# An offset of its own in the schedule's keys for each of a group's 16 steps

## Chip, cores and metric

The kernel runs on one core of a Trainium2 chip. The metric is the time of one execution on the device in microseconds (us). Of the kernel before there are three runs: 2164.63, 2165.2 and 2167.5 us; the median is 2165.2.

## What is computed

The input is a batch of 128 graphs of 64 nodes with 512 features each, and a weighted adjacency matrix of 64x64 for each graph. Four layers follow one another, each of the form x = layernorm(x + layer(x, adj)):

```python
# layer 0: A = exp(leaky(8 tanh((s_i + s_j) / 8))) * adj, rows normalized; A @ x @ w
# layer 1: softmax-like attention over the graph: adj * exp(q k^T), rows normalized, times v
# layer 2: w_i = q_i . (adj @ k)_i / sqrt(512); softmax over the graph; times v
# layer 3: hypergraph convolution 512 -> 1024, relu, layernorm, hypergraph convolution 1024 -> 512
x = _layernorm(x + _L0_gnn_ref(x, adj, L0_gnn_w, L0_gnn_a), axis=-1)
x = _layernorm(x + _L1_gnn_ref(x, adj, ...), axis=-1)
x = _layernorm(x + _L2_gnn_ref(x, adj, nodemask, L2_gnn_Wqk, L2_gnn_Wv), axis=-1)
x = _layernorm(x + _L3_gnn_ref(x, adj, ...), axis=-1)
```

All of it is in fp32.

## The kernel before

Two graphs make a tile of 128 rows, two tiles a group; there are 32 groups, and two groups share a chunk of adjacency data. A group goes through all four layers without leaving the chip: only x comes in and the result goes out. The products with the weights are made by Strassen's scheme (seven half-size products, `seven_products`, with the sums of the left side made by DVE in `side_sums`); the weight pieces are prepared once, stored in DRAM, and streamed back for every group into a ring of eight buffers of 512 KB.

The kernel does not write instructions in the order of its code. `run(g)` (line 1004) only records operations with `order.add` (line 76): the engine, an estimated cost, what is read and written, and a key. `step(k)` (line 1006) sets the key for the operations of the 16 steps of a group, numbered 0 to 15: layer 0 is steps 0 to 2 (scores and their exponentials, the gather over the graph, the products), layer 1 is 3 to 6, layer 2 is 7 to 11, layer 3 is 12 to 15. `BASE[g]` sets the groups apart by 4 key units, so that the 16 units of one group overlap those of the next three.

`keys_by_what_follows` (line 105) then replaces the step by a finer one: an operation's place is computed from the longest chain of work that follows it in its group, on a scale of 16 units. What the operation had been given ahead of its step is kept: `urgent` (100 for `NOW`, the operations that empty a PSUM bank, 1.5 for the weight streams) and `early`:

```python
        o.engine, o.cost, o.emit, o.key, o.step = engine, cost, emit, self.key - urgent - self.early, self.key
                urgent = o.step - o.key
                o.key = o.step - urgent
```

`Order.run` (line 140) is a list scheduler. It keeps, for each engine, a heap of the operations whose inputs are ready by its own estimate, and takes the one with the lowest key for which buffers are free: 14 of the kind k4 (activations), 8 of the ring, 8 PSUM banks, 7 of e and so on, each a stack of free numbers. It allows eight DMAs under way (`UNDERWAY`), and a group's loads no further than `AHEAD` in front of the work. For TensorE `choose` (line 122) also looks at the tiling mode: some matmuls use the whole array, others four quarters of 64x64 (`mode="quarters"`: the gathers over a graph) or two columns (`mode="columns"`: the scores); it stays in a mode while the keys are not too far apart. The sum over a graph (`over_graph`, line 968) may be written whole or in halves, as the mode just then is.

The order in which operations are taken is then the order in which they are emitted, and it is fixed for every engine by dependencies between neighbours (`pinned`, line 1172). Each engine works through its own queue strictly in that order, and SyncE, which issues every DMA, too. So the keys decide, before anything runs, in what order each of the five queues stands, and which buffer number each operation uses. All instructions carry the line of this helper, 1178, in the profile; they are told apart by the names of their buffers.

Before the change, only the operations of step 0 have an offset: `EARLY = 1.0`, set in `run` around step 0 and taken back ahead of step 1.

The first group also prepares the weights: `prepare_first` makes the pieces of w0 and of layer 1's v in the ring buffers, uses them in place for group 0, and stores them to DRAM; from group 1 on `streamed` loads them from there.

Of the kernel before, what the change touches and what calls it, by code (L numbers as in the profile page):

```python
# [28 lines left out]
BASE = [APART * g - 2 * min(g, 4) - 2 * max(g - NG + 3, 0) for g in range(NG)]  # L29
# [29 lines left out]
class Order:  # L59
# [4 lines left out]

    NEAR, FAR = 0.5, 4.0
    ENOUGH = 48
    EARLY = 1.0

    BLOCK, REST = 64, 3500
    AHEAD = 3.5  # L70
# [189 lines left out]
def kernel(  # L260
# [51 lines left out]
    order = Order({k: len(v) for k, v in kinds.items()})  # L312
# [10 lines left out]
    def dve(n, reads, writes, emit, urgent=0.0, port=None):  # L323

        if port is None:
            port = all((b[0] if isinstance(b, tuple) else b).kind != "bank" for b in reads)
        order.add("DVE", w_dve(n), reads, writes, emit, urgent, port=port)
# [55 lines left out]
    def load_x(g):  # L383
        order.key = (-11.0, -10.3)[g] if g < 2 else BASE[g] - 6.0
        xs[g] = Buf("x", 4)
        load(xs[g], x_g[g], P * GT * D * 4)

    def load_adj(c):
        order.key = BASE[GC * c] - 7.0 if c else -10.5
        adjs[c] = Buf("adj")  # L390
        load(adjs[c], adjT[:, ts(c, CT * N)], P * CT * N * 4, lambda t_: t_.rearrange("p t i -> p (t i)"))

        turned = turned_adjs[c] = Buf("adj", 2 * GT)
        order.key += 0.0 if c else 0.6
        for t in range(GT):
            for h in range(2):
                dma(P * 256, [], [turned[2 * t + h]],
                    lambda t=t, h=h: turned.t[ts(t, N)].rearrange("p (g h) i -> p g h i", h=2)[:, :, h],
                    lambda t=t, h=h: adjT_c[c, t][:, :, h])
# [604 lines left out]
    def run(g):  # L1004

        def step(k):
            order.key, order.group = BASE[g] + float(k), g

        step(0)
        xt = xs.pop(g)  # L1010
        adj, turned, gm, am, sums, g1, dc, dh = prepared[g // GC]
# [2 lines left out]
        of_x = lambda t: xt[[2 * t, 2 * t + 1]], lambda t: xt.t[:, t, :]  # L1014


        order.early = order.EARLY
        s = Buf("col", GT)
        diag, e, ps_s = Buf("e", GT), Buf("e", GT), Buf("bank")
        for t in range(GT):  # L1020
# [4 lines left out]
        for t in range(GT):  # L1025
# [8 lines left out]
        rs = Buf("e")  # L1034
        dve(7 * GT * N, [ps_e], [rs], lambda: nc.vector.reciprocal(flat(rs.t), ps_e.t[:, : GT * N]), NOW)
        dve(GT * N, [e, rs], [e], lambda: nc.vector.tensor_mul(e.t, e.t, rs.t))
        order.early = 0.0
        step(1)
        left = left_side(gathered(*of_x, lambda h, t: e.t[halves[h][0], t, :], [e]))
        step(2)  # L1040
        seven_products(*left, first_use["w0"] if g == 0 else streamed("w0"), *scaled_into(
            at_x, sums, slice(2 * CT + own.start, 2 * CT + own.stop), D // 2))
# [116 lines left out]
    for g in range(NG):  # L1159
        if g:  # L1160
            load_x(g)
        if g % GC == 0:
            if g:
                load_adj(g // GC)
            prepare_chunk(g // GC)
        run(g)
        order.group = None


    last, names, behind = {}, {}, []  # L1170
# [78 lines left out]
```

## Time and profile before

| what | value |
|---|---|
| median of three runs | 2165.2 us (2164.63 to 2167.5) |
| the profiled execution's own time | 2166.22 us |
| its span, first to last instruction | 2164.4 us |
| TensorE, mean granted clock | 0.998 |
| instructions | 51412 |
| DMA traffic | 476.34 MB, mean 220 GB/s |

The profile is of one execution. "PE" is TensorE's matmuls, "PEld" its weight loads, which lie beside the matmuls; "SPq" is SyncE's queue, which issues the DMAs. An fp32 matmul stands as two records, so a product of 256 columns over two blocks of 128 rows is four records of 128x256. Buffer names tell what an operation is for:

| out<-in | what it is |
|---|---|
| bank<-ring,k and bank<-ring,h | products with a streamed weight piece |
| bank<-k,m | products with the two Gram matrices m1 and m2 that stay on chip |
| bank<-ident,x | transposes |
| bank<-e,x, bank<-kept,x, bank<-kept,h | gathers over a graph, in quarters |
| bank<-k,k 128*64 | scores, in columns |
| bank<-k,k 128*128 | making of the Gram matrices, at the start only |
| bank<-e,same | sums over a graph |

The costliest groups of TensorE, with their number, busy time and mean duration of one:

| group | number | busy us | mean ns |
|---|---|---|---|
| bank<-ring,k 128x256 | 3456 | 801.3 | 382 |
| bank<-k,m 128x128 | 3584 | 437.0 | 276 |
| bank<-ring,k 128x512 | 512 | 237.6 | 598 |
| bank<-ring,h 128x256 | 1024 | 235.2 | 380 |
| bank<-ring,h 128x512 | 384 | 176.8 | 594 |
| bank<-kept,h 64x64 | 4096 | 74.1 | 221 |
| bank<-k,k 128x64 | 2048 | 74.2 | 225 |

Matmuls overlap in the records, since each is drawn from its start to its modelled end; so the mean durations are longer than the distance from one start to the next.

### The profile page before, as it was taken

Reading aid. Unit: us, or ns where it says so; the run is one execution under the profiler, and the core shown is the slowest. Engines: PE = TensorE matmul, PEld = TensorE weight load, DVE = VectorE, ACT = ScalarE, POOL = GpSimd, SP = SyncE. Lnnn points to the kernel's source line nnn. Section 1 sums busy time; section 2 is a strip of 40 time slices with the busy share of each in tenths; the row PEclk is TensorE's granted clock in tenths of the full one; section 3 lists DMA queues with packets and bytes.
Section 4 is the critical chain, followed back from the end, with each engine's and each line's share of the span. In section 5 each row is a group of like instructions: output and inputs, shape, how many; then the busy total and the mean of one; then the engine's idle time right before and its main releaser. Section 6 shows DMA issues by size and latency. Waiting matters only on the chain.

```text
span 2164.4 us, 51412 instructions
## 1 busy us (share of the span) xinstructions
PE 2142.8 (99%) x20831; PEld 1717.2 (79%) x20831; DVE 1541.9 (71%) x3967; ACT 856.9 (40%) x1812; POOL 386.1 (18%) x399
## 2 busy tenths in 40 slices
PE   7999999999999999999999999999999999999998
PEld 4887777887888787887878887878877888878866
DVE  6777767677776776776777776777766777766675
ACT  2444343343433433443433434434334333343433
POOL 1113121021201212101222111212012211012120
PEclk9999999999999999999999999999999999999999
DMA  8866668666666667665666665666666666655475
GB/s 276 309 217 224 210 203 282 224 218 235 223 210 205 207 218 240 212 218 198 204 234 220 226 200 207 212 235 224 212 203 210 221 232 213 212 189 207 160 256 198
DMA packets 174364, 476.34 MB, mean 220 GB/s; under 512 B 35824, under 2 KB 45360, under 8 KB 174128
## 3 DMA queue, kind: packets, MB, share of 16 engines
q1 hardware_dynamic: 174128, 473.05, 64.4%
q8 instruction: 165, 2.70, 0.5%
q14 instruction: 71, 0.58, 0.1%
HBM read 443.33 MB, written 29.66 MB: 219 GB/s over the span
## 4 chain that ended last, share of the span: by engine, by line
PE 97%; DMA 2%; DVE 0%; ACT 0%; SPq 0%; issue 0%; POOL 0%; POOLq 0%; DVEq 0%; ACTq 0%
PE bank L1178 97%; DMA x<-in_x_dram 0%; DMA k<-in_wk_dram 0%; DMA ring<-in_wv_dram 0%; DMA k<-in_wqk_dram 0%; DMA v<-ring 0%; DMA ring<-w 0%; SPq L1178 0%; ACT k L1178 0%; DVE k L1178 0%; ACT x L1178 0%; DVE x L1178 0%; DVE col L1178 0%; POOL ring L1178 0%; POOLq L1178 0%
## 5 line engine op out<-in xcount | busy, mean ns | idle before, releaser
L1178 PE MATMUL bank<-ring,k 128*128 128x256 f32 (+1 forms) x3968 | 1035.4, 410 | 7.0 <-DMA ring<-w 4.9
L1178 PEld LDWEIGHTS bank<-ring,k 128*128 128x128 f32 x3968 | 730.3, 190 | 211.3 <-issue 111.2
L1178 ACT COPY k<-bank 128x512 f32<-128x512 f32 (+1 forms) x640 | 304.6, 501 | 603.3 <-PE bank L1178 405.7
L1178 DVE SCALAR_TENSOR_TENSOR x<-bank,col,x 128x256 f32<-128x256 f32 (+1 forms) x832 | 400.7, 500 | 198.8 <-PE bank L1178 187.4
L1178 PEld LDWEIGHTS bank<-k,m 128*128 128x128 f32 x3584 | 427.2, 192 | 22.2 <-issue 13.5
L1178 PE MATMUL bank<-k,m 128*128 128x128 f32 x3584 | 437.0, 276 | 0.0
L1178 PE MATMUL bank<-ring,h 128*128 128x256 f32 (+1 forms) x1408 | 412.0, 439 | 0.0
L1178 POOL TENSOR_TENSOR col<-col,mhalf 128x2 f32<-128x2 f32 (+1 forms) x161 | 111.4, 692 | 1476.8 <-DVE col L1178 634.0
L1178 PEld LDWEIGHTS bank<-ring,h 128*128 128x128 f32 x1408 | 260.1, 190 | 90.0 <-issue 64.3
L1178 ACT ACTIVATE x<-x,col,col 128x512 f32<-128x512 f32 x256 | 197.3, 809 | 168.7 <-DVE col L1178 168.5
L1178 DVE TENSOR_TENSOR k<-bank,k 128x256 f32<-128x256 f32 x384 | 154.0, 421 | 129.1 <-PE bank L1178 123.2
L1178 DVE BATCH_NORM_STATS2 col<-x 128x6 f32<-128x512 f32 x256 | 175.3, 688 | 4.5
L1178 DVE SCALAR_TENSOR_TENSOR h<-bank,col,b3a_b 128x512 f32<-128x512 f32 x128 | 95.9, 750 | 70.5 <-PE bank L1178 69.9
L1178 ACT ACTIVATE k<-bank,u_c 128x128 f32<-128x128 f32 x256 | 80.0, 364 | 133.2 <-PE bank L1178 131.7
L1178 ACT ACTIVATE h<-h 128x512 f32<-128x512 f32 x128 | 80.6, 631 | 127.5 <-DVE h L1178 127.4
L1178 ACT ACTIVATE h<-h,col,col 128x512 f32<-128x512 f32 x128 | 96.8, 807 | 73.6 <-DVE col L1178 73.6
L1178 DVE TENSOR_TENSOR k<-k 128x256 f32<-128x256 f32 x226 | 95.8, 425 | 41.0 <-ACT k L1178 40.6
L1178 PEld LDWEIGHTS bank<-k,k 128*64 128x64 f32 (+1 forms) x2112 | 77.3, 140 | 51.4 <-DVE k L1178 24.2
L1178 PE MATMUL bank<-k,k 128*64 128x64 f32 (+1 forms) x2112 | 105.7, 237 | 6.7 <-DMA k<-in_wk_dram 4.8
L1178 DVE SCALAR_TENSOR_TENSOR h<-bank,col,h 128x512 f32<-128x512 f32 x128 | 93.3, 748 | 22.7 <-PE bank L1178 20.6
L1178 POOL TENSOR_TENSOR x<-x,bv_b 128x512 f32<-128x512 f32 x64 | 81.1, 1271 | 92.0 <-PE bank L1178 68.4
L1178 POOL TENSOR_TENSOR k<-k,b3b_b 128x512 f32<-128x512 f32 x64 | 81.3, 1270 | 79.1 <-DVE k L1178 31.4
(96 smaller groups left out, 1494.4 us busy)
## 6 DMA issues: line engine op xcount, KB each, us to landing
ring<-3a SPq DMA_DIRECT2D x224, 512.0 KB, 4.6
ring<-3b SPq DMA_DIRECT2D x224, 512.0 KB, 4.4
ring<-v SPq DMA_DIRECT2D x189, 512.0 KB, 3.8
ring<-w SPq DMA_DIRECT2D x93, 512.0 KB, 3.3
x<-in_x_dram SPq DMA_DIRECT2D x32, 512.0 KB, 4.6
ring<-v SPq DMA_DIRECT2D x63, 256.0 KB, 4.0
out_dram<-x SPq DMA_DIRECT2D x31, 512.0 KB, 3.0
ring<-w SPq DMA_DIRECT2D x31, 256.0 KB, 4.1
```

The lines of the kernel that those rows point to most:

```text
L1178: made = f(*args, **kwargs)
```

## The change

The single offset becomes a list of 16, one for each step. `step(k)` sets it together with the key; the two lines that set and cleared it around step 0 go, and it is set to 0 after each group, so that the loads and the preparation of chunks, which are recorded between the groups, have none, as before. A positive offset lowers the keys of a step's operations, so that they are taken earlier among those ready; a negative one raises them.

```diff
-    EARLY = 1.0
+
+    EARLY = [2.22, 0.44, 0.0, 0.0, 0.0, 0.0, 0.0, 0.17, 0.0, 0.57, -0.17, -0.03, -1.1, -0.36, 0.0, -0.35]
...
         def step(k):
-            order.key, order.group = BASE[g] + float(k), g
+            order.key, order.early, order.group = BASE[g] + float(k), order.EARLY[k], g
...
-        order.early = order.EARLY
         s = Buf("col", GT)
...
         dve(GT * N, [e, rs], [e], lambda: nc.vector.tensor_mul(e.t, e.t, rs.t))
-        order.early = 0.0
         step(1)
...
         run(g)
-        order.group = None
+        order.early, order.group = 0.0, None
```

Nothing else differs: the operations, their costs in the scheduler, the buffers and their numbers are the same.

## The prediction

> **What bounds the kernel now.** I read the page's busy line and its chain first, then the idle time of TensorE by what ended it, then one table of six stretches, then the timeline at the start and the end.
>
> ```profile
> PE 2142.8 (99%) x20831; PEld 1717.2 (79%) x20831; DVE 1541.9 (71%) x3967; ACT 856.9 (40%) x1812; POOL 386.1 (18%) x399
> PE 97%; DMA 2%; DVE 0%; ACT 0%; SPq 0%; issue 0%; POOL 0%; POOLq 0%; DVEq 0%; ACTq 0%
> ```
>
> TensorE is busy 2142.8 of 2164.4 us and the chain is TensorE's own for 97%. The next engine, DVE, is at 71%.
>
> ```profile
> PE bank L1178 <- DMA ring<-w: 4.9, 1, 4.9
> PE bank L1178 <- DMA k<-in_wk_dram: 4.8, 2, 4.1
> PE bank L1178 <- DMA k<-in_wqk_dram: 1.8, 1, 1.8
> PE bank L1178 <- ACT k L1178: 1.7, 3, 1.2
> ```
>
> The six stretches (us, then busy time and instructions of PE, PEld, DVE, ACT, POOL, then clock, DMA share, GB/s):
>
> ```profile
> 0.00:62.00 62.00, 49.45 (x334) 28.86 (x335) 36.81 (x104) 16.77 (x49) 11.09 (x17) 0.94 0.87 286
> ...
> 400.00:1000.00 600.00, 600.00 (x5903) 484.38 (x5902) 430.80 (x1114) 237.20 (x498) 106.13 (x110) 1.00 0.65 218
> ...
> 2100.00:2165.00 65.00, 55.66 (x550) 42.22 (x548) 39.69 (x84) 22.54 (x36) 8.93 (x10) 0.98 0.58 197
> ```
>
> The first block holds TensorE's waits of over 1 us in total. In the stretches the second number after the colon is TensorE's busy time: 600.00 of 600.00 us in the steady part, 12.5 us short in the first 62, 9.3 short in the last 65, of which 7.7 lie after the last matmul's end at 2157.3 (0.6 of it beyond the span). A new order of the same work can therefore gain only at the two ends, and on whatever the steady 2000 us contain besides matmuls: changes of tiling mode.
>
> The timeline of TensorE at the start (start us, us, what, idle before it):
>
> ```profile
> 49.02 1.13 PE L1178 MATMUL bank<-ring,k 128*128 128x256 f32 x4
> 55.02 2.04 PE L1178 MATMUL bank<-ring,k 128*128 128x256 f32 x4 [4.86 <-DMA ring<-w]
> 56.85 0.63 PE L1178 MATMUL bank<-e,same 128*128 128x128 f32 x2
> 57.97 2.71 PE L1178 MATMUL bank<-ring,k 128*128 128x256 f32 x8 [0.48 <-DVE k L1178]
> 60.52 1.04 PE L1178 MATMUL bank<-ident,x 128*128 128x128 f32 x8
> ```
>
> The chain at the same place (start us, us, what), and the last matmuls of the timeline:
>
> ```profile
> 35.28 6.92 DMA ring<-in_wv_dram
> ...
> 42.45 1.70 POOL ring L1178
> ...
> 44.16 5.33 DMA v<-ring
> ...
> 49.51 0.59 SPq L1178
> ...
> 50.21 4.67 DMA ring<-w
> ```
>
> ```profile
> 2130.05 0.69 PE L1178 MATMUL bank<-kept,h 64*64 64x64 f32 x32
> 2131.96 1.99 PE L1178 MATMUL bank<-ring,k 128*128 128x256 f32 x8 [1.22 <-ACT k L1178]
> ```
>
> In the timeline TensorE stands 4.9 us before group 1's first product, until the weight piece w0 is back from DRAM at 54.88. The chain tells why that load is so late: the DMA queue on SyncE goes on only at 49.51, when the store of the v pieces has landed. In the last two lines a gathered block goes straight into a product, which waits for ACT's copy of it.
>
> **What the Trainium skill says.** "TensorEngine Tiling (Array Packing)", Key Properties: a change of tiling mode drains TensorE. The trace agrees, in start-to-start intervals: a 128x256 matmul takes 216 ns before another of its kind and 309 before one on divided tiles (+93); the last 64x64 one takes 148 ns before an undivided one, 38 before another divided shape (+110); columns to quarters is 152 against 38 (+114). "Perfetto Trace Analysis", Identifying the Most-Contended Engine: matmul busy share does not tell the distance to the roofline. It holds here too: a matmul of 382 ns mean starts every 216, so I count intervals, not busy time. "DMA: Bandwidth & Descriptors", Anatomy of one DMA: DMA engines don't wait on semaphores, the issuing sequencer does; the waiting SyncE queue at 44.16 to 49.51 is such a case.
>
> **The change, part by part.** No work is added or removed. By instruction count ACT (1814), DVE (3901), POOL (404) and SyncE (1073) hold the same number in both programs, TensorE one fewer: one over-graph sum more is written whole instead of as two halves. What moves is the order on all five queues, everywhere: step 0 of a group is keyed 2.22 early (1.0 before), step 1 0.44 and step 9 0.57 early, step 12 1.1 late, 13 and 15 some 0.35 late. A key's unit is a quarter of a group, about 17 us of TensorE (2120 us by 32 groups by 4). I price it where TensorE's time can change.
>
> 1. Mode changes. Counted in the two orders: before, 132 entries into divided tiles, 132 exits, 68 changes between columns and quarters; after, 131, 131 and 63. That is 93 + 110 + 5 x 114 = 773 ns. Gain 0.8 us.
>
> 2. The start. SyncE's first 36 issues are the same, and the 18 between there and the first reload of w0 are the same transfers in another order, behind the same v store (which needs POOL's 1.70 us at 42.45). One difference: the fourth x load now stands behind that store instead of ahead of it, and the reload eight transfers behind the x load, where the trace of before shows the queue standing for a transfer of about that distance. I put the landing 0.6 us later, at 55.5 (bounds: 0 and 1.2). What TensorE does ahead of it grows by four transposes (8 records x 112 ns = 0.9 us) and some small sums, together 1.0 us. Is that work ready? The w0 product that stood at 49.02 moves ahead of the last Gram matrix, to about 45; from its end, two DVE evictions (0.88), statistics (0.69 + 0.18 + 0.17), POOL's power (0.72), DVE's product and ACT's normalization (0.8 for a tile), with the DVE work queued between, end near 52.6; transposing ends before 54. Yes. After the landing, before loses 0.34 at 55.57, 0.79 at 57.97 and 0.37 at 58.56 because operands of group 1 come from DVE late; in the new order the transposes and a gather stand there and DVE's side sums are several instructions earlier. I take all of these 1.5 us as gone (bounds 0.5 and 1.5). Gain 1.0 + 1.5 - 0.6 = 1.9 us. The earlier offset also frees the adjacency buffer for chunk 1's load, which before used a fresh one: its last reader, DVE's product for group 1, now comes near 30 us, the load at 36, so SyncE doesn't wait.
>
> 3. The steady part. Before has no wait there, so nothing can go; new ones can come. The ring of eight weight buffers has one tight place in the new order: near 327 and 333 us the same ring buffer is reloaded with 4.7 and 4.3 us of matmuls between its last use and its next. A load costs a wait of 0.1 to 0.3, an issue, and a median of 3.3 to 4.6 us to landing from the page's issue table: 4.9 taken. Loss 0.2 + 0.6 = 0.8 us (bounds 0 and 2). Beyond it TensorE's operands have as much matmul work between maker and user as before, mostly more. DVE at 71% and POOL at 18% are reordered beneath that cover; if the cover failed, each late operand would cost about the 0.4 to 1.2 us that such waits cost at the ends.
>
> 4. The end. In the new order five products (1.7 us each) stand between the gather of group 62 and the product that reads it: the 1.28 us at 2131.96 go. What is late next: group 63's last gather now follows its last 3a product after six products, 10.4 us, where before it had 12.4. The chain in between (two evictions to +1.8, relu to +2.9, statistics waiting behind residual adds to +7.1, POOL to +8.05, ACT's four pieces from +8.35, 0.73 each) has its first piece at +9.2 and the last at +11.3; the gather reads them at 10.4 to 12.0. It holds, by some 0.3 us for the second piece. The 7.1 us after the last matmul have the same instructions. Gain 1.3 us (bounds 0.6 and 1.7).
>
> Sum: -0.8 - 1.9 + 0.8 - 1.3 = -3.2 us. The profiled execution took 2166.22 (span 2164.4), 1.0 over the median of 2165.2; against the median 2165.2 - 3.2 = **2162.0**, 0.15% less. A measurement of this kernel can tell about 0.2% (4.3 us) from no change.
>
> **Rivals.**
> A, the forecast, 2162.0, chance 0.57, own range 2160.5 to 2164.
> B, the reload of w0 is earlier: if it need not wait for the x load or the store, SyncE could issue it when it reached it, near 47.9 instead of 50.2. Then 2.3 + 0.6 more are gained: 2162.0 - 2.9 = 2159.1. For: its own data were stored long before. Against: the chain shows the queue standing, and the transfers ahead are the same. Chance 0.22.
> C, the start gives nothing: the landing slips 1.2 us and new short operand waits follow it. 2162.0 + 1.9 + 0.6 = 2164.5. For: DVE is full there (36.8 of 62 us), and one of its v subtractions now stands ahead of three evictions and waits for a load. Chance 0.14.
> D, slower: the ring loads fall behind in every group, not in one place. Steps 13 and 15 start their streams with 0.35 less lead; if one load a group is late by the 0.3 us that separate a 4.6 us landing from the tight gap, 28 steady groups lose 8.4: 2162.0 + 8.4 = 2170.4. It decides from 7.5 us in sum, or 0.27 a group. Against: loads and their users are shifted by the same offset, steady DMA share is 0.65, and before has not one ring wait after 55 us. Chance 0.07.
> That the change does nothing is excluded: the planner recomputes each key from what follows but keeps the offset, and the orders differ from the first matmuls of group 1 on.
>
> **How the numbers follow.** Faster: B and the lower edge of A, 0.22 + 0.04 = 0.26. Slower: D, 0.07. Same: 0.67. The range runs from below B, 2158.5, to 2166: C and A's bad bounds (2162.0 + 1.2 + 1.0 + 0.7 + 0.6 = 2165.5) are in it, D is out.
>
> **What would show it.** Mode changes: 325 in the trace. Start: the wait for the w piece is still the longest of TensorE, between 54.5 and 56, with transposes ahead of it, and nothing over 0.4 us behind it. Steady: short waits on the ring near 330 us and nowhere regularly. End: no wait of over 0.5 us after 2100. A regular wait in the steady part, or a w piece that lands before 53, would make the forecast wrong.

## The result, and the profile after

| | before | after |
|---|---|---|
| median | 2165.15 us (10 runs, 2164.63 to 2167.5) | 2159.56 us (10 runs, 2157.94 to 2163.08) |
| ratio to before, 95% interval | | 0.9973 (0.9965 to 0.9982) |
| profiled execution, span | 2166.22, 2164.4 us | 2158.29, 2156.5 us |
| changes of tiling mode in the trace | 332 | 325 |

The kernel is 5.6 us faster, 0.26%, and the interval of the ratio does not reach 1. The two profiled executions differ by 7.9 us: before's lies 1.0 over its median and after's 1.3 under its own. So some 2 us of what follows belong to the two executions and not to the change.

Busy line and chain of the kernel after:

```profile
PE 2139.4 (99%) x20829; PEld 1721.0 (80%) x20829; DVE 1529.5 (71%) x3967; ACT 861.1 (40%) x1812; POOL 385.7 (18%) x399
PE 97%; DMA 2%; DVE 0%; SPq 0%; ACT 0%; issue 0%; DVEq 0%; ACTq 0%
```

TensorE is still the bound, and its busy time fell by 3.4 us for the same matmuls. That is the first oddity: another order can take waits away, but why should the matmuls themselves get shorter? TensorE's waits of the kernel after (us in total, times, longest):

```profile
PE bank L1177 <- DVE e L1177: 1.7, 1, 1.7
PE bank L1177 <- DMA ring<-w: 1.5, 1, 1.5
PE bank L1177 <- DMA k<-in_wqk_dram: 1.3, 1, 1.3
PE bank L1177 <- DVE k L1177: 0.6, 1, 0.6
```

The wait for group 1's piece of w0 went from 4.9 us to 1.5, a wait of 1.7 us for DVE is new, and the last wait of over 1 us for ACT's copy is gone. The first and the last stretch (us, busy time and instructions of PE, PEld, DVE, ACT, POOL, then clock, DMA share, GB/s):

```profile
0.00:62.00 62.00, 52.35 (x428) 32.01 (x429) 39.17 (x113) 19.52 (x56) 11.98 (x18) 1.00 0.90 295
...
2100.00:2157.00 57.00, 49.40 (x435) 37.45 (x433) 33.59 (x76) 17.67 (x27) 7.70 (x9) 0.98 0.62 209
```

The number to look at is the clock: 1.00 in the first 62 us, where the same stretch of before had 0.94. That digit stood in the prediction's own fence and was not read. The timeline of TensorE at the start (start us, us, what, idle before it):

```profile
47.94 1.11 PE L1177 MATMUL bank<-e,x 64*64 64x64 f32 x60
50.75 0.44 PE L1177 MATMUL bank<-e,same 64*64 64x128 f32 x4 [1.70 <-DVE e L1177]
51.12 0.66 PE L1177 MATMUL bank<-ident,x 128*128 128x128 f32 x4
53.23 1.13 PE L1177 MATMUL bank<-ring,k 128*128 128x256 f32 x4 [1.45 <-DMA ring<-w]
54.20 0.60 PE L1177 MATMUL bank<-ident,x 128*128 128x128 f32 x4
```

One standstill of 4.9 us has become two of 1.7 and 1.5, with a sum over a graph and four transposes between them. The four matmuls with w0 take 1.13 us; in the kernel before the same four took 2.04. The end of the timeline:

```profile
2134.95 2.10 PE L1177 MATMUL bank<-kept,h 64*64 64x64 f32 x128
2137.27 3.72 PE L1177 MATMUL bank<-ring,k 128*128 128x256 f32 x16 [0.23 <-ACT k L1177]
```

The wait of 1.28 us behind a gather is gone, and the last gather costs 0.23, as it did before.

To see why matmuls got shorter, the clock has to be read in finer stretches. Before, from 52 to 60 us:

```profile
52.00:56.00 4.00, 0.98 (x2) 0.83 (x3) 2.25 (x7) 0.55 (x2) 0.72 (x1) 0.58 0.88 286
56.00:60.00 4.00, 3.52 (x11) 2.72 (x10) 2.08 (x7) 2.21 (x5) 0.00 (x0) 0.57 0.95 358
```

After, the same stretches:

```profile
52.00:56.00 4.00, 2.77 (x73) 2.39 (x74) 2.39 (x6) 1.06 (x3) 1.97 (x2) 1.00 1.03 370
56.00:60.00 4.00, 4.00 (x23) 3.65 (x23) 2.52 (x7) 2.24 (x6) 1.27 (x1) 1.00 0.98 357
```

In the kernel before, TensorE was granted half its clock from 52.63 to 59.46 us: from inside the long wait to 4.4 us behind it. A 128x256 matmul there starts 427 ns after the one before it, where the usual distance is 216 ns. Added up over the matmuls of that piece this is 1.9 us, besides 0.8 us of a wait for DVE among them. The profile of after has no such piece until its matmuls have ended. Another 0.6 us of the 3.4 is the half clock with which every execution begins: it lasted to 8.26 us before and to 7.24 after, while TensorE's first 49 matmuls stand in the same order in both kernels, so this part is no gain of the change.

The Trainium skill describes this under "TensorE: Matmul & The Clock Gate", What's actually happening: the clock is set half or full by how busy the array was in a free-running window of 3413 ns. The traces agree on the window: in this case's runs half-speed pieces between the start and the end last 3.41, 6.83 or 10.24 us, one to three windows. They differ on what sets it off. The page says an idle window; here windows in which TensorE was busy for up to 46% of the time (counted from its records) were followed by half speed, another of 46% and all above it were not, and a half-speed window had to be busy for somewhere between 81% and 86% for full speed to come back.

### The profile page after: what moved, and what is told of

Its sections match the earlier page's. It is cut to its first block, busy times and chain, and to the rows that moved or that the text cites. A ratio compares the mean times of both kernels' runs of the same rounds, so it can differ in the third digit from the quotient of the medians.

```text
span 2156.5 us, 51432 instructions
## 1 busy us (share of the span) xinstructions
PE 2139.4 (99%) x20829; PEld 1721.0 (80%) x20829; DVE 1529.5 (71%) x3967; ACT 861.1 (40%) x1812; POOL 385.7 (18%) x399
## 4 chain that ended last, share of the span: by engine, by line
PE 97%; DMA 2%; DVE 0%; SPq 0%; ACT 0%; issue 0%; DVEq 0%; ACTq 0%
PE bank L1177 97%; DMA x<-in_x_dram 0%; DMA k<-in_wk_dram 0%; DMA mask_rows<-e 0%; DMA k<-in_wqk_dram 0%; DMA ring<-in_wv_dram 0%; DMA ring<-w 0%; SPq L1177 0%; DVE x L1177 0%; DVE col L1177 0%; DVE ring L1177 0%; ACT x L1177 0%; DVE e L1177 0%; ACT k L1177 0%; DVE k L1177 0%
## 5 line engine op out<-in xcount | busy, mean ns | idle before, releaser
L1177 PEld LDWEIGHTS bank<-k,m 128*128 128x128 f32 x3584 | 432.8, 192 | 30.5 <-issue 19.9
L1177 PE MATMUL bank<-k,m 128*128 128x128 f32 x3584 | 445.9, 276 | 0.0
L1177 PE MATMUL bank<-ring,h 128*128 128x256 f32 (+1 forms) x1408 | 421.8, 440 | 0.0
L1177 DVE BATCH_NORM_STATS2 col<-h 128x6 f32<-128x512 f32 x128 | 87.3, 686 | 20.2 <-ACT h L1177 20.0
```

The source lines that it names most:

```text
L1177: made = f(*args, **kwargs)
```

## The experiments

Before and the variants were timed on the same chip in each of three sessions; before's medians there were 2165.54, 2165.09 and 2165.20 us. Each ratio is to before beside it. "Waits" below is the sum of all delays of over 60 ns in TensorE's starts, against the usual distance for that pair of matmuls, in one profile; matmuls at half clock count in it.

### Where the gain lies: the start, the middle and the end alone

Three kernels use the new list for some groups, and before's offset for the others:

```diff
-            order.key, order.early, order.group = BASE[g] + float(k), order.EARLY[k], g
+            order.key, order.group = BASE[g] + float(k), g
+            order.early = order.EARLY[k] if g <= 3 else float(k == 0)
```

In the second the condition is `g >= 28`, in the third `4 <= g <= 27`.

> The new offsets in groups 0 to 3 only, the single offset of 1.0 in the rest. Theory (the gain is mostly the start: less waiting of TensorE up to 62 us): 330 mode changes (0.2 us less than before), the start as in the changed kernel (3 to 4 us less), the end as before with its wait of 1.2 us: 2161.5 us. Rival (the gain is in the steady part, or in the mode changes alone): nothing to speak of is gained in four groups, 2164.9 us.

> The new offsets in groups 28 to 31 only. Theory: the start as before, 334 mode changes (0.2 us more), the wait of 1.2 us near the end gone because five products stand between the gather and its reader: 2164.0 us. Rival (the end is worth more than its one wait): 2162 us or less. Rival (the steady part): 2165.2 us.

> The new offsets in groups 4 to 27 only; the first 163 rows of TensorE's order are those of before, and the end again has the gather read at once. Theory: 329 mode changes, 0.3 us less, and nothing else: 2164.8 us. Rival (the steady part holds the gain): 2160 us. A new late ring load in the steady part would show as over 2165.5 us.

| new list for | median us | ratio (95%) | waits, first 60 us | waits, 2100 to 2150 us |
|---|---|---|---|---|
| groups 0 to 3 | 2165.65 | 1.0004 (0.9996 to 1.0012) | 11.4 | 2.5 |
| groups 28 to 31 | 2163.02 | 0.9990 (0.9983 to 0.9997) | 10.8 | 0.6 |
| groups 4 to 27 | 2165.47 | 0.9996 (0.9988 to 1.0005) | 12.4 | 2.3 |
| all (after) | 2159.56 | 0.9973 (0.9965 to 0.9982) | 8.4 | 0.6 |
| none (before) | | | 13.8 | 2.4 |

The two columns of waits are of one execution each: that for groups 0 to 3 took 3.6 us more than its kernel's median, the next two took 1.5 and 1.4 less than theirs. And 3.5 to 5.1 us of the waits of the first 60 us (5.1 before, 3.5 after) lie ahead of TensorE's 50th matmul, near 25 us, up to which its order is the same in all five. At both ends the groups also stand closer than was described: `BASE` sets the first five, and the last three, 2 units apart and not 4, so an offset is a larger share of their distance there.

The end is as predicted in kind: the 1.28 us go with the last four groups alone. The middle does nothing that can be measured. The start alone missed its theory by 4 us and met the rival, but not for the rival's reason: its trace shows a loss elsewhere. Timeline of TensorE in that kernel:

```profile
169.87 1.12 PE L1178 MATMUL bank<-k,ones 128*128 128x512 f32 x2 [1.12 <-DVE k L1178]
172.36 1.68 PE L1178 MATMUL bank<-k,m 128*128 128x128 f32 x8 [1.37 <-DVE k L1178]
```

and the stretch behind it, with the clock as third number from the end:

```profile
173.00:176.00 3.00, 3.00 (x16) 3.00 (x16) 1.59 (x6) 1.12 (x2) 0.00 (x0) 0.50 0.84 343
```

At 170 us DVE still prepares layer 3's weights, once. TensorE's order leaves that of the kernel after at 89 us, ahead of this preparation, DVE's operands came late twice, and the half clock followed: 5.7 us of waits between 160 and 300 us, where before has 1.3. So the experiment had made a loss of its own, though this execution, 3.6 us over the median, shows more of it than most.

### The start alone, with the seam elsewhere

As the first, with `g <= 6`: TensorE's order is then that of the kernel after until well behind that preparation.

> The new list for groups 0 to 6 only; the others keep 1.0 for step 0 and nothing for the rest. The seam between the two lists then lies behind the one-time preparation of layer 3's weights near 170 us, and TensorE's order up to there is that of the kernel after. 326 changes of tiling mode by count. Theory (the new order's gain at the start is real, and in the start experiment the seam ate it): the first 62 us lose 4 to 5.5 us less to waits than before's 13.8, no wait of over 0.5 us between 100 and 300 us, the 1.28 us at the end stay; time 2165.3 - 2.4 - 0.5 = 2162.4. Rival (what the profiles show at the start is transfers that happened to land early): about 2165.

Measured: 2162.31 us, ratio 0.9988 (0.9981 to 0.9995), 2.8 us under before. The theory's time came to 0.1 us; there is no wait of over 0.5 us between 100 and 300 us. But the waits of the first 60 us were 11.7 in its profile, only 2.1 less than before's, because this execution, 2.3 us over its kernel's median, had the half clock, from 53.62 to 60.45 us. So the new order of the start does not keep the half clock away for certain: of the four profiles that share it, the two of after are without, and this one and the first experiment's have it. Parts add up: by the ratios, start 2.6, middle 0.9 and end 2.2 us make 5.7, for 5.8 of the whole, each part to about 1.6 us and with groups 4 to 6 in two of them.

### Which offsets make the start

```diff
-    EARLY = [2.22, 0.44, 0.0, 0.0, 0.0, 0.0, 0.0, 0.17, 0.0, 0.57, -0.17, -0.03, -1.1, -0.36, 0.0, -0.35]
+    EARLY = [2.22, 0.0, 0.0, 0.0, 0.0, 0.0, 0.0, 0.0, 0.0, 0.0, 0.0, 0.0, 0.0, 0.0, 0.0, 0.0]
```

> The list with step 0's 2.22 alone, all other steps at 0. 327 changes of mode by count. Theory (the start is step 0's doing, since a group's first gathers and transposes are what fills TensorE while group 1's w0 piece is on its way): waits in the first 60 us at most 9.5 us, where before has 13.8 and after 8.4; time 2162 if the end stays as before, 2161 if its wait goes too. Rival (the other 15 offsets are needed): 2165 or more, with regular waits or more than one stall of over 1 us behind 100 us.

And the other 15 alone:

```diff
-    EARLY = [2.22, 0.44,
+    EARLY = [1.0, 0.44,
```

> The new list with step 0 put back to 1.0. The order of TensorE's first 45 us is that of the kernel before, but there are 352 changes of mode instead of 332. Theory (the start comes from step 0, and a change of mode costs about 0.1 us): the start loses as much as before's 13.8 us, the 20 more changes cost 2.0 us: 2167.3 if the end's wait stays, 2166.0 if it goes. Rival (the other offsets carry the gain): 2163 or less.

Step 0 alone: 2164.15 us, 0.9995 (0.9987 to 1.0003), no change that can be told, and 13.8 us of waits in the first 60, as many as before. The theory that the start is step 0's doing fell, and the rival's 2165 was not reached either. The timeline of that kernel, in its slowest execution, 3.5 us over the median:

```profile
53.60 0.49 PE L1177 MATMUL bank<-e,same 128*128 128x128 f32 x2 [1.89 <-DVE e L1177]
56.23 2.05 PE L1177 MATMUL bank<-ring,k 128*128 128x256 f32 x4 [2.14 <-DMA ring<-w]
59.05 1.99 PE L1177 MATMUL bank<-e,x 64*64 64x64 f32 x64 [0.78 <-DVE e L1177]
```

The two waits of the kernel after stand here too, but with little between them, and one of 1.4 us for ACT stands ahead of them at 48.09: at 54.20 the half clock sets in and lasts three windows, to 64.44. Two of the 13 executions kept a mean clock of 0.999, and they took 2159.78 and 2161.08 us. The others alone: 2168.99 us (2167.0 to 2170.4, one execution of 5642.56 apart), 1.0016 (1.0009 to 1.0024). Its start waits 13.3 us, as before's, and its 20 more mode changes at about 0.1 us would make 2.0 of the 3.5 us lost by the ratio; the rest was not traced to a place. It takes both, a lead for step 0 and the other steps' offsets: by the ratios they give 5.8 us together, 1.1 and a loss of 3.5 alone. That the others help by putting work between the waits is read from these profiles, and no run shows it by itself.

### Taking the wait for w0 away

Group 1 uses the w0 pieces where they were made, as group 0 does; first in the kernel after, then in the kernel before:

```diff
-        seven_products(*left, first_use["w0"] if g == 0 else streamed("w0"), *scaled_into(
+        seven_products(*left, first_use["w0"] if g <= 1 else streamed("w0"), *scaled_into(
```

> The changed kernel, with group 1 also using the w0 pieces in place in the ring, so that its first product doesn't wait for a reload from DRAM. Theory (that reload is the last thing that TensorE waits for at the start): its wait of 1.5 us at 53 us goes, 329 mode changes cost 0.4 more: 2158.5 us. Rival (DVE's exponential rows at 50.7 and its left sides are late next, the reload only hides it): the wait moves, 2159.6 us or a little more.

> The kernel before, with group 1 also using the w0 pieces in place instead of loading them back from DRAM. 330 changes of mode. Theory (the wait for w0 hides late work of DVE behind it, as with the new list, where keeping w0 gave 1.7 us of the 1.6 us wait but left 1.75 of waits for DVE): the wait of 5 us goes, some 1.5 us of waits for DVE come, time 2165.3 - 3.5 = 2161.8. Rival (the wait is all that holds the start): the whole 5 us and the short waits behind it go, 2159.5 or less, and the new list would have been worth less than one kept piece.

> The kernel after with group 1 using the w0 pieces in place, once more, beside the kernel after on the same chip. Theory (without the wait for w0 the half clock cannot come): 2157.9, all executions within 2157 to 2159.5 and at a clock of 0.999, 1.5 less than the kernel after beside it. Rival (its few executions were lucky ones): a spread like that of after, and a median within 0.5 of it.

With the new list: 2157.84 us, 0.9962 (0.9950 to 0.9975), and again 2158.17, 0.9969 (0.9957 to 0.9981). In both profiles no reload is waited for, and the product with w0 waits 1.16 us for ACT instead (for ACT, where the expectations had DVE): a wait came in its place, as the rival said, but the time is the theory's, as is the clock. With the old list: 2163.9, 0.9994 (0.9986 to 1.0003), 2 to 4 us short of both expectations. Timeline of the old list with w0 kept, in an execution 1.9 us over the median:

```profile
49.76 3.77 PE L1178 MATMUL bank<-ring,k 128*128 128x256 f32 x15
56.72 0.49 PE L1178 MATMUL bank<-e,same 128*128 128x128 f32 x2 [3.18 <-ACT e L1178]
57.04 5.31 PE L1178 MATMUL bank<-ring,k 128*128 128x256 f32 x16
```

The wait of 5 us is gone, and behind it stands one of 3.2 us for a sum over a graph, which ACT releases; the half clock follows (58.07 to 61.48), and so 16 matmuls take 5.31 us instead of 3.6. In the kernel before the same sum stands at 56.85 us behind w0's product and waits for nothing: its operands were made ready under the wait for w0. Taking that wait away gave 1.2 us of its 5 by the medians, which the interval does not tell from nothing.

### Keeping TensorE busy inside the wait

Matmuls that nothing uses are put where TensorE stands, in a bank that no operation holds just then. In the kernel before, 16 of them ahead of group 1's first product with w0:

```diff
-    for o in order.run():
+    planned = order.run()
...
+    for i, o in enumerate(planned):
+        if i in fills:
+            for _ in range(fills[i][1]):
+                nc.tensor.matmul(fills[i][0][:, :P], ident, ident, start=True, stop=True)
```

> The kernel before, with 16 matmuls of the identity with itself (128x128, into a PSUM bank that is free) on TensorE directly ahead of group 1's first product with the reloaded w0, that is, inside the wait of 5 us; their results are used by nothing. In the profile of before the granted clock is half from 52.63 to 59.46 us, that is, from inside this wait to 4.5 us behind it, and the same is seen in every other profile behind a stretch of 3.4 us in which TensorE was busy for less than about 46%. Theory (the long wait costs twice: the wait itself, and half speed behind it): the piece of w0 lands when it did, at about 54 to 55 us, but there is no half clock between 45 and 70 us and the 0.34 and 0.37 us between the first products behind the wait are gone; 2165.3 - 2.3 = 2163.0. Rival (the products behind the wait are late because of DVE, as the prediction said): those pieces stay, and the time is 2165.3 or, with work added, more.

Measured: 2163.74 us, 0.9994 (0.9986 to 1.0002). By time alone this is not told from no change; by the clock the effect is plain. Of its 13 executions 11 have a mean granted clock of 0.999, of the 24 of before beside it 2 have. Timeline:

```profile
48.84 3.73 PE L1178 MATMUL bank<-ident 128*128 128x128 f32 x32
53.38 1.10 PE L1178 MATMUL bank<-ring,k 128*128 128x256 f32 x4 [0.81 <-DMA ring<-w]
54.31 0.39 PE L1178 MATMUL bank<-e,same 128*128 128x128 f32 x2
55.39 1.99 PE L1178 MATMUL bank<-ring,k 128*128 128x256 f32 x8 [0.69 <-DVE k L1178]
```

and its stretch from 56 us:

```profile
56.00:60.00 4.00, 4.00 (x25) 3.59 (x24) 2.18 (x5) 2.23 (x5) 2.05 (x2) 1.00 1.02 365
```

The piece still lands after 53 us, but the four products with it take 1.10 us instead of 2.04 and the next eight 1.99 instead of 2.71: the clock is full. Of the three delays that the prediction blamed on DVE, the 0.34 and the 0.37 have shrunk to 0.08 and 0.10 and the 0.79 is there, as 0.85. The first two were the clock for the most part, the third is DVE.

The clocks of single executions give a price in time as well. Each execution has its mean clock on record, and 0.999 or more leaves room for one window of half clock at most, since 3.41 us at half are 0.0008 of 2160 us:

| | at 0.999 or more | median us | below | median us |
|---|---|---|---|---|
| before, all three sessions | 11 of 117 | 2163.75 | 106 | 2165.40 |
| before, with the 16 matmuls | 11 of 13 | 2163.57 | 2 | 2165.32 |
| new list for groups 0 to 6 | 9 of 20 | 2161.83 | 11 | 2163.85 |
| after, both sessions | 13 of 17 | 2158.90 | 4 | 2160.94 |

In each of these rows the executions at the lower clock are 1.6 to 2.0 us longer, and the change makes them rare. But at the higher clock after is still 4.8 us faster than before, of 5.6 in all. So the half clock is about 1 us of the change, and most of the gain lies elsewhere. Executions were sorted here and not made, so this is a comparison and not an experiment.

In the kernel after, six such matmuls stand ahead of each of the two waits:

> The kernel after, with six such unused matmuls of the identity in each of its two waits there: ahead of the over-graph sum that waits 1.9 us for DVE, and ahead of group 1's first product with w0 (1.6 us). Two more changes of mode (0.2 us), inside the wait. Theory (the spread of the kernel after, 2157.9 to 2163.1, is the clock: in some executions a 3.4 us stretch holds both waits and the half clock follows): no execution has the half clock, all lie under 2160.5, median 2158.9. Rival (the spread is the arrival of transfers): as wide as without, median 2159.6 or more.

> The kernel after, unchanged, beside the others on this chip. Theory: median 2159.6; executions with a mean granted clock of 0.999 lie at about 2158.9, those with 0.998 at about 2161.7. Rival (the clock follows the time and not the other way): no such step, and the same time at either clock.

With them 2159.49 us (2157.62 to 2163.23), beside it the kernel after as it is, 2159.29 (2157.13 to 2160.55). No execution of the first is below a clock of 0.999, and the spread stayed, with the longest at a clock of 1.000; and of the second the one at 0.998 took 2159.36. So the half clock makes part of before's start and some of after's long executions, but not the whole spread: the 13 executions of after at 0.999 or more alone reach from 2157.13 to 2160.55. What makes that spread stays open. One piece of it shows in the profile of the filled kernel:

```profile
335.64 1.53 PE L1177 MATMUL bank<-ring,k 128*128 128x512 f32 x3 [0.28 <-DMA ring<-3a]
```

This is the ring's tight place, 0.45 us against the usual distance; in the two profiles of the kernel after it cost under 0.1.

## Why the prediction was right, and where not

The direction, the two places and the range held: 2159.56 lies in 2158.5 to 2166.0, and 2.4 us under the forecast of 2162.0. It is also under that forecast's own range, which began at 2160.5. A gain of over 4.3 us, the size from which the prediction held a gain to be told from no change, had a chance of 0.26 in it, against 0.67 for less; it came.

1. Mode changes, 0.8 us: the count is exact, 325, six of the seven fewer within the first 400 us. The steady part got nothing: from group 6's column-sum product to group 27's before takes 1380.75 us and after 1381.60 and 1381.82, with 210 changes there before and 208 after. What makes the 0.9 to 1.1 us more was not found.

2. The start, 1.9 us: the step that failed is its reason. The prediction took the delays behind w0's landing, 1.5 us, as operands late from DVE; only the 0.79 was that. The other 0.7 was part of the half clock, 1.9 us in all in that profile, which the forecast did not know. "Is that work ready? Yes" was wrong for the sums over a graph, of which one waits 1.7 us for DVE.

Its term "the landing 0.6 later" can't be told: in four profiles with each order of the first 60 us (before, end, middle and the other 15 offsets; after twice and both starts) group 1's w0 product starts 29.9 to 30.9 and 29.4 to 31.4 us behind the product for which layer 2's first weights are needed, 30.4 and 30.6 on average. What the new reload waits for is as forecast: it was issued at 48.59 us, when the x load eight transfers ahead had landed, at 48.53. But the chain of before was misread. SyncE's queue did not stand from 44.16 to 49.51:

```profile
46.39 1.47 SPq L1178 DMA_DIRECT2D v<-ring  x2
47.91 2.20 SPq L1178 DMA_DIRECT2D adj<-in_adjT_dram  x3
50.21 0.54 SPq L1178 DMA_DIRECT2D ring<-w  x1
```

It issued seven more transfers in that stretch, and stood 0.3 us for the x load (landed at 48.81) and under 0.1 us for the v store.

By size the start came out near the forecast. Behind the 50th matmul the four profiles with each order have 8.2 and 6.0 us of waits up to 60 us, so 2.2 less; but with the new order these are 3.8 and 4.9 us in the two profiles with the full clock and 7.5 and 7.7 in the two with the half clock. The ratio of groups 0 to 6 gives 2.6 us, where 1.9 and six mode changes, together 2.5, were said. Executions of like clock give 1.9 and 1.6 us, so the rarer half clock is the smaller part of it. That the sums agree so well is in part luck, since one reason failed and the half clock was not in the sum.

3. The ring near 330 us, 0.8 us lost: it is the right place, but in four of the five profiles with the full list (after and after with w0 kept, each twice) it costs 0.2 us or less, and in the filled one 0.45. The term was too large.

4. The end, 1.3 us: the wait is gone in all of these, and the delays between 2100 and 2150 us fell from 2.4 to 0.6, so 1.8, just above the bound of 1.7. The last four groups alone gave 2.2 us by the ratio, with an interval that holds 1.3. Ring and end, with about 0.8 and 0.5 us, are thus the terms that explain a part of the 2.4 us by which the forecast fell short; the intervals of the parts, 1.6 us each way, do not allow more.

Rival B had the right number, 2159.1, by luck: SyncE did issue the reload at 48.59 instead of 50.21 us, but everything in that profile was 1.4 us earlier from 23 us on, and the reload did wait for the x load. C and D did not come; no regular wait exists in the steady part. Of the signs named, the longest wait at the start was to be the one for w0, between 54.5 and 56: it came at 53.2, and the one for DVE is longer. A piece that lands before 53 us was named as a sign against the forecast; it landed at 53.18 in the first profile of after and at 51.88 in the second.

The fastest kernel seen is after with w0 kept for group 1, 1.7 us under after's first median and 1.1 under after beside it; the intervals do not separate the two.

## What to carry to other kernels

Read the clock column before explaining a slow matmul: a stretch whose clock is under 1.00 explains in one number what otherwise looks like many late operands, and a long wait on TensorE can be charged twice, once as the wait and once behind it. Then compare executions of like clock, before the clock is taken for the cause of the whole gain: here it was about 1 us of 5.6. Where a wait cannot be shortened, spreading work into it so that no window of 3.4 us is less than half busy may pay by itself: here 1.9 us by the trace and 1.5 by the medians, which the interval does not tell from nothing. An experiment that gives one part of a change a seam must be read in its trace, since the seam can cost as much as the part gains.

## What the hardware showed that was not expected

The windows of the clock have another phase in each execution: TensorE starts its first matmul at 4.1 to 4.3 us in every profile, and full speed comes at 7.1 to 10.3. So does the half speed behind a wait: it was one window in three places (the end alone, the old list with w0 kept, the seam at 170 us), two in five profiles (before, the middle, both starts, the 15 other offsets) and three with step 0 alone; and none in six (after twice, after with fill, after with w0 kept twice, before with fill).

TensorE also stands for 0.08 or 0.10 us every 13 us on average in the steady part, at uneven distances, in every kernel, some 2 us for each 300 us, without a releaser in the trace; no run here was made to find out what it is.
